# Layer 0 of a four-layer graph network: relation rows of three slots in four by one-hot matmuls, wider compares, one strided sum

## The chip, the cores and the metric

The kernel runs on one core of one Trainium2 chip, as one launch. The metric is the device time in microseconds. The engines and their names in the profile are TensorE (PE, its weight loads PEld), VectorE (DVE), ScalarE (ACT), GpSimd (POOL) and SyncE (SP). Each takes its own instructions in order; they meet at semaphores.

## What is computed

The reference is four graph layers in a row over 3125 nodes of 128 features and 100,000 edges sorted by target. After each of them the node features are added and normalized. The change is in layer 0, of which this is the core (`hP1` to `zWz` are small matrix products):

```python
z_edge = z[edge_type]                                  # 500 relations, 64 features
z_bar = segment_sum(z_edge, dst) / maximum(deg, 1)
pre_self = hP1 + hP2 + z_bar @ P3
pre_edge = hP1[dst] + hP2[src] + zP3[edge_type]
logits = leaky(pre) @ y_w                              # 8 heads, of edges and of nodes
alpha = softmax of the logits over all that arrive at one node
t_edge = hWh[src] + zWz[edge_type]
out = leaky(segment_sum(alpha * t, dst) + residual_weight * h)
```

So each edge needs a row that belongs to its source (`hP2`, `hWh`) and a row that belongs to its relation (`zP3`, `zWz`, and `z` itself for the mean). Layer 1 is a mean over neighbours, which the kernel computes with a matrix of edge counts; those counts are made inside layer 0's loop.

## The kernel before

**Tiles and slots.** The nodes are ordered by falling degree and cut into 25 tiles of 128, one node to a partition. Tile t has `CAP[t]` slots, 57 down to 21, 821 in all; a slot is one incoming edge of each of the 128 nodes. Slots are worked in chunks of up to W = 8, so a tile has some whole chunks and mostly a partial one, 114 in all.

**A chunk.** Both kinds of chunk first gather, by GpSimd, one row of 264 numbers per edge from `h_tab` into `hs` (L90, called at L824 and L841; one indirect DMA a slot; `hs` has 8 buffers). Then they differ:

- `gathered` (L819): GpSimd gathers a second row of 328 numbers per edge from `z_tab` into `zs` (two buffers). VectorE adds it to `hs` (L826), sums the relations' 64 features over the slots by halves (L814, L817) and adds the sum to `za` (L828). TensorE then builds the argument `pre` of the logits by matmuls with the identity (L799, L833).
- `multiplied` (L837): SyncE loads the relation numbers of 8 slots, repeated over the partitions, into `rb` (L843, two buffers). For each half of the chunk and each of the NK = 4 groups of 128 relations VectorE compares 512 columns with the group's relation numbers (L852), which makes a one-hot `oh`. TensorE multiplies it with `zq`, the relation table as a sum of three bf16 parts (L854, two matmuls for each one-hot, one PSUM buffer `zps`). ScalarE copies the result to `zT` (L856). TensorE adds it to `pre` (L858), adds `hs` (L860), and makes the value part `t_ps` three slots at a time (L866, one PSUM buffer); VectorE adds that to `hs` (L867). At the end VectorE sums `zT` over the 8 slots by halves (L870, L814, L817) and adds it to `zbT` (L874).

In both, `logits` copies `pre` with a ReLU (L806, ScalarE) and multiplies by `yw8` (L808).

**Which chunk is of which kind.** `by_matmul` (L68) takes n whole chunks of a tile, spread evenly, with n/full near 9/20 of all slots: 47 chunks, for instance the first and the third of four. 445 slots are gathered.

**End of a tile.** VectorE masks the logits (L881), takes the softmax, and `spread` (L885) weighs each chunk's `hs` and sums it; only then are the tile's `hs` buffers free. A chain of small steps closes the tile: the row x1 is scattered by GpSimd to `x1_tab` (L93) and `u` is written to `u_tab` (L1008).

**Counts.** `counts` (L563) is a generator whose steps are woven between the chunks: VectorE makes pairs of one-hots `c_ohs` and `c_ohd` (L559) for a piece of 512 columns, TensorE multiplies them block by block (L634) into `c_ps`, ScalarE copies it (L636). `NB[t]`, the blocks of ends per 128 columns, is 3 in the first 3 tiles, 2 in the next 21 and 1 in the last; a piece has 4 x NB blocks, at most SE = 12.

**Order.** The program's order within a queue is not quite that of the code: the framework lays the instructions out. In the trace the GpSimd queue holds the `hs` gathers of several chunks one after the other, then the load of x, the scatter of x1, and then the `zs` gathers.

Of the kernel before, what the change touches and what calls it, by code (L numbers as in the profile page):

```python
# [8 lines left out]
F32 = mybir.dt.float32  # L9
F16 = mybir.dt.float16  # L10
BF16 = mybir.dt.bfloat16
I32 = mybir.dt.int32
AF = mybir.ActivationFunctionType
OP = mybir.AluOpType
AX = mybir.AxisListType
# [3 lines left out]
P = 128  # L19
# [8 lines left out]
W = 8  # L28
# [6 lines left out]
R = 64  # L35
HC = 2 * D + H
NK = (PADREL + 1) // P
# [3 lines left out]
CAP = [57, 42, 40, 39, 38, 37, 36, 35, 35, 34, 33, 33, 32, 31, 31, 30, 30, 29, 28, 28, 27, 26, 25, 24, 21]  # L41
# [9 lines left out]
NB = [3] * 3 + [2] * (NT - 4) + [1]  # L51
CW = 512
# [15 lines left out]
def by_matmul(t):  # L68

    full = CAP[t] // W  # L70
    n = (9 * CAP[t] + 10 * W) // (20 * W)
    return {i * full // n * W for i in range(n)}


# [1 line left out]
def tile_gnn(ctx, tc, a, out):  # L76
    nc = tc.nc
    V, A, G, T = nc.vector, nc.scalar, nc.gpsimd, nc.tensor
# [10 lines left out]
    def gather(dst, table, idx, **kw):  # L89
        return G.indirect_dma_start(out=dst, out_offset=None, in_=table, in_offset=indirect(idx), **kw)  # L90
# [35 lines left out]
    relid = const.tile([P, NK], F32, name="relid")  # L126
# [223 lines left out]
    zq = slots.tile([P, NK, 4 * R], BF16, name="zq")  # L350
# [135 lines left out]
    with tc.tile_pool(name="srcp", bufs=1) as sp, tc.tile_pool(name="srcq", bufs=2, space=PSUM) as ps:  # L486
# [8 lines left out]
        for t in range(NT):  # L495
# [6 lines left out]
                                   op0=OP.add, op1=OP.mult)  # L502
            V.scalar_tensor_tensor(srcs[:, sl], pay_sb[:, sl, 0], float(-NP), live[:, :CAP[t]],
                                   op0=OP.add, op1=OP.mult)
# [10 lines left out]
        for o in range(0, NS, P):  # L515
            n = min(P, NS - o)
# [15 lines left out]
        blk0[nb] = late.tile([P, NT], F32, name=f"blk0_{nb}")  # L532
        G.iota(blk0[nb], pattern=[[nb * P, NT]], base=0, channel_multiplier=0, allow_small_or_imprecise_dtypes=True)
    SG = 8
    SE = max(NB) * CW // P
    each_j = slots.tile([P, NT, max(CAP)], BF16, name="each_j")
    V.tensor_copy(each_j, digits[:, :NT].unsqueeze(2).to_broadcast([P, NT, max(CAP)]))
    NAX = NT * max(NB)
# [1 line left out]
    def count_up(pool, ps):  # L540

        up = ps.tile([P, P, 2], BF16, name="c_up")
        of = up.rearrange("p d s -> p (d s)")
        ri = pool.tile([P, 1], I32, name="c_ri")
        V.tensor_copy(ri, rowid)
        V.tensor_scalar(ri, ri, 1, None, op0=OP.arith_shift_right)
        rf = pool.tile([P, 1], F32, name="c_rf")
        V.tensor_copy(rf, ri)
        for k in range(2):
            row = pool.tile([P, P], BF16, name="c_row", bufs=2)  # L550
            V.tensor_scalar(row, onesb, rf, float(k * P // 2), op0=OP.mult, op1=OP.add)
            T.transpose(of[:, k * P:(k + 1) * P], row, identb)
        return up

    def one_hots(to, nums, n, up):

        for i, k, w in ((0, n // 2, 2), (n - n % 2, n % 2, 1)):
            if k:
                V.tensor_tensor(to[:, i // 2:i // 2 + k, :, :w], nums[:, i:i + k * w]  # L559
                                .rearrange("p (b w) -> p b w", w=w).unsqueeze(2).to_broadcast([P, k, P, w]),  # L560
                                up[:, :, :w].unsqueeze(1).to_broadcast([P, k, P, w]), op=OP.is_equal)

    def counts(t, cp, ps, up):  # L563


        n, nb = CAP[t], NB[t]
        NA = NT * nb
        sl = slice(OFF[t], OFF[t + 1])
        oh = cp.tile([P, NT * max(CAP)], BF16, name="c_oh")[:, :NT * n]
# [7 lines left out]
        end = cp.tile([P, NT + 1], F32, name="c_end")  # L577
# [24 lines left out]
        for s0 in range(0, n, SG):  # L602
            k = min(SG, n - s0)
# [11 lines left out]
            for s in range(k):  # L615
                T.matmul(perm, ohb[:, s // 2, :, s % 2], oha[:, s].rearrange("p e a -> p (e a)"), start=(s0 + s == 0),
                         stop=(s0 + s == n - 1))
        ends = cp.tile([P, 2, NAX + NAX % 2], BF16, name="c_ends")
# [2 lines left out]
        cs = cp.tile([P, NP], BF16, name="c_sb")  # L621
        for c in range(NCW):
            w = min(CW, NP - c * CW)
            n2, e0 = nb * w // P, nb * CW // P * c
            yield
            ohs = cp.tile([P, SE // 2, P, 2], BF16, name="c_ohs", bufs=2)
            ohd = cp.tile([P, SE // 2, P, 2], BF16, name="c_ohd", bufs=2)
            for to, end in ((ohs, 0), (ohd, 1)):
                one_hots(to, ends[:, end, e0:e0 + n2], n2, up)
            cps = ps.tile([P, CW], F32, name="c_ps")  # L630
            for j in range(w // P):
                for i in range(nb):
                    b = nb * j + i
                    T.matmul(cps[:, j * P:(j + 1) * P], ohd[:, b // 2, :, b % 2], ohs[:, b // 2, :, b % 2],  # L634
                             start=(i == 0), stop=(i == nb - 1))
            A.activation(cs[:, c * CW:c * CW + w], cps[:, :w], AF.Copy)  # L636
        yield
        od_ps = ps.tile([P, NT], F32, name="c_od", tag="c_ps")
# [115 lines left out]
    with tc.tile_pool(name="l0", bufs=2) as wp, tc.tile_pool(name="l0s", bufs=1) as sp, \  # L754
# [40 lines left out]
        def argument(hq, k):  # L795

            pre = ps.tile([P, 4, P], F32, name="pre")
            for i in range(3):
                T.matmul(pre[:, :k], hq[:, i, :], identb.unsqueeze(1).to_broadcast([P, k, P]), start=(i == 0),  # L799
                         stop=False)  # L800
            return pre

        def logits(pre, k, lg_ps):

            low = wp.tile([P, 4, P], F32, name="low")
            A.activation(low[:, :k], pre[:, :k], AF.Relu)  # L806
            for s in range(k):
                T.matmul(lg_ps[:, s, :], low[:, s, :], yw8, start=True, stop=True)  # L808

        def halved(v, n, last=None):  # L810

            while n > 2:
                k = n // 2
                V.tensor_add(v[:, :k], v[:, :k], v[:, n - k:n])  # L814
                n -= k
            if n == 2:
                V.tensor_add(v[:, 0] if last is None else last, v[:, 0], v[:, 1])  # L817
# [19 lines left out]
        def multiplied(hq, o, n, zbT, first, lg_ps):  # L837

            hs = wp.tile([P, W, HC], F32, name="hs", bufs=8)
            for s in range(n):  # L840
                gather(hs[:, s, :], h_tab, srcx[:, o + s:o + s + 1])  # L841
            rb = wp.tile([P, W * P], F16, name="rb")
            nc.sync.dma_start(rb[:, :n * P], rel_tab[o:o + n].rearrange("(o s) p -> o (s p)", o=1)  # L843
                              .to_broadcast([P, n * P]))
            zT = wp.tile([P, W * P], F32, name="zT")
            for s0 in range(0, n, 4):
                k = min(4, n - s0)
                cols = slice(s0 * P, (s0 + k) * P)
                oh = wp.tile([P, NK, 4 * P], BF16, name="oh")[:, :, :k * P]
                zps = ps1.tile([P, 4 * P], F32, name="zps")[:, :k * P]  # L850
                for i in range(NK):
                    V.tensor_scalar(oh[:, i], rb[:, cols], relid[:, i:i + 1], None, op0=OP.is_equal)  # L852
                    for k2 in range(2):
                        T.matmul(zps, zq[:, i, 2 * R * k2:2 * R * (k2 + 1)], oh[:, i], start=(i + k2 == 0),  # L854
                                 stop=(i == NK - 1 and k2 == 1))
                A.activation(zT[:, cols], zps, AF.Copy)  # L856
                pre = argument(hq, k)
                T.matmul(pre[:, :k], zw[:, :D], zT[:, cols], start=False, stop=False)  # L858
                for s in range(k):
                    T.matmul(pre[:, s, :], hs[:, s0 + s, :D], ident, start=False, stop=(s == k - 1))  # L860
                logits(pre, k, lg_ps[:, s0:s0 + k])
            for s0 in range(0, n, 3):
                k = min(3, n - s0)
                t_ps = ps1.tile([P, 3, HC - D], F32, name="t_ps")
                for s in range(k):
                    T.matmul(t_ps[:, s, :], zT[:, (s0 + s) * P:(s0 + s + 1) * P], zw[:, D:], start=True, stop=True)  # L866
                V.tensor_add(hs[:, s0:s0 + k, D:], hs[:, s0:s0 + k, D:], t_ps[:, :k])  # L867
            assert n == W
            zh = wp.tile([P, W // 2, P], F32, name="zh")
            V.tensor_add(zh, zT.rearrange("z (s p) -> z s p", p=P)[:, :W // 2],  # L870
                         zT.rearrange("z (s p) -> z s p", p=P)[:, W // 2:])
            halved(zh, W // 2, zbT if first else None)
            if not first:
                V.tensor_add(zbT, zbT, zh[:, 0])  # L874
            return hs

        def masked(lg_ps, hss, n, mk):
# [28 lines left out]
        up = count_up(cp, ps1)  # L906

        def all_counts():
            for t in range(NT):
                yield from counts(t, cp, ps1, up)  # L910
# [6 lines left out]
        for t in range(NT):  # L917
            n = CAP[t]
# [5 lines left out]
            zbT = wp.tile([P, P], F32, name="zbT")  # L924
            hss = []
            mults = by_matmul(t)
            for s0, w in chunks(t):
                o = OFF[t] + s0
# [83 lines left out]
    with ExitStack() as ctx1, tc.tile_pool(name="l1", bufs=2) as wp, tc.tile_pool(name="l1s", bufs=1) as sp:  # L1012
# [14 lines left out]
        with tc.If(general > 0):  # L1027

            with tc.tile_pool(name="l1g", bufs=1) as gp, tc.tile_pool(name="l1gp", bufs=1, space=PSUM) as ps:
# [13 lines left out]
                for t in range(NT):  # L1043
# [27 lines left out]
                    for c in range(NCW):  # L1071
                        w = min(CW, NP - c * CW)
# [5 lines left out]
                for c in range(NCW):  # L1078
                    w = min(CW, NP - c * CW)
# [24 lines left out]
        for c in range(NCW):  # L1104
            w = min(CW, NP - c * CW)
# [11 lines left out]
            for i in range(w // P):  # L1117
                j = c * (CW // P) + i
# [26 lines left out]
    with tc.tile_pool(name="l2", bufs=2) as wp, tc.tile_pool(name="l2s", bufs=1) as sp, \  # L1145
# [100 lines left out]
        for t in range(NT):  # L1246
            qp = query(ps1, qb[:, t, :])
            for s0, s1, run in segments(t):
# [5 lines left out]
                n, o = s1 - s0, OFF[t] + s0  # L1254
# [46 lines left out]
    with tc.tile_pool(name="l3", bufs=2) as wp, tc.tile_pool(name="l3s", bufs=1) as sp, \  # L1301
# [28 lines left out]
        for t in range(NT):  # L1330
            n = CAP[t]
# [38 lines left out]
```

## Time and profile before

| what | value |
|---|---|
| median of 3 runs | 4815.34 us (4812.5 to 4819.78) |
| the profiled execution, its own time | 5636.56 us |
| its span, first to last instruction | 5634.8 us |
| mean granted TensorE clock in it | 0.619 |

The profiled execution is a run of its own and takes longer than the others. The span falls into five stages; the busy times are microseconds:

| from, to (us) | what | PE | DVE | ACT | POOL |
|---|---|---|---|---|---|
| 0, 330 | tables, order of the nodes, first gathers | 154 | 185 | 42 | 105 |
| 330, 2865 | layer 0, the loop over tiles | 1370 | 1337 | 647 | 1327 |
| 2865, 3080 | layer 1 | 146 | 54 | 26 | 30 |
| 3080, 4390 | layer 2 | 350 | 742 | 151 | 801 |
| 4390, 5635 | layer 3 | 6 | 642 | 62 | 806 |

How to read the profile: a group line has source line, engine, operation, output and inputs by the program's names with their shapes and a count; then busy microseconds and the mean nanoseconds of one; then the engine's idle time just before these instructions and what ended most of it. In the stage table each busy time is followed by the number of instructions, and the last columns are the granted TensorE clock, the DMA engines' busy share and GB/s. A wait line has the engine and what waited, what ended the wait, and then total microseconds, times, and the longest.

### The profile page before, as it was taken

What the parts mean: (1) busy time and instruction counts of PE and PEld (TensorE: products, weight loads), DVE (VectorE), ACT (ScalarE), POOL (GpSimd) and SP (SyncE); (2) the same over time, 40 slices, a digit from 0 to 9 for tenths busy, and PEclk for the clock granted to TensorE, in tenths of its full rate; (3) what the DMA queues carried; (4) which work ended last, traced back from release to release, by engine and by line L of the source; (5) the groups of instructions that cost most, each with busy time, mean ns of one, the idle gap of its engine ahead of it and who ended that gap; (6) DMA issues with size and microseconds to landing.
All of it is one profiled execution on the core that took longest, in us unless ns stands there. A gap on an engine that the chain in (4) does not pass through costs nothing. (4 is left out here: it accounts for less than half of the span.)

```text
span 5634.8 us, 37936 instructions
## 1 busy us (share of the span) xinstructions
PE 2025.8 (36%) x10974; PEld 1311.2 (23%) x11061; DVE 2959.0 (53%) x6784; ACT 927.9 (16%) x2462; POOL 3069.7 (54%) x3137
## 2 busy tenths in 40 slices
PE   7164554556544555555564022222233100000000
PEld 5143433334333444334432010111111000000000
DVE  8354664555544655555432455555566354555555
ACT  1032222222222322222111011111111000000000
POOL 0545566454554445444503756666564476666665
PEclk9576766666676777776677555555555555555555
DMA  2423333332233333323343333333332233333322
GB/s 82 124 73 91 93 93 96 86 90 75 77 91 84 83 86 88 89 82 84 101 170 119 105 96 105 104 103 114 98 109 84 81 100 91 89 89 95 94 85 68
DMA packets 220244, 530.70 MB, mean 94 GB/s; under 512 B 65689, under 2 KB 112460, under 8 KB 215385
## 3 DMA queue, kind: packets, MB, share of 16 engines
q0 software_dynamic: 147968, 437.97, 27.6%
q1 hardware_dynamic: 72024, 89.90, 4.9%
q8 instruction: 94, 1.54, 0.1%
q14 instruction: 158, 1.29, 0.1%
HBM read 457.09 MB, written 70.63 MB: 94 GB/s over the span
## 5 line engine op out<-in xcount | busy, mean ns | idle before, releaser
L90 POOL DMA_INDIRECT hs<-h_tab,srcx x821 | 880.3, 1072 | 666.2 <-issue 534.7
L90 POOL DMA_INDIRECT kv<-kv_tab,pay_sb x821 | 783.6, 954 | 423.9 <-issue 241.1
L90 POOL DMA_INDIRECT kv<-ktv_tab,pay_sb x821 | 780.2, 950 | 336.0 <-issue 256.1
L90 POOL DMA_INDIRECT zs<-z_tab,rel x445 | 458.0, 1029 | 451.6 <-DVE az L828 141.6
L706 DVE TENSOR_REDUCE u<-msg 128x128 f32<-128x1024 f32 (+4 forms) x228 | 384.3, 1686 | 114.5 <-remote 61.6
L808 PE MATMUL lg<-yw,low 128*128 128x8 f32 x1642 | 243.5, 274 | 126.2 <-ACT low L806 72.2
L634 PE MATMUL c_ps<-c_ohs,c_ohd 128*128 128x128 bf16 x1300 | 139.5, 264 | 406.3 <-issue 193.9
L808 PEld LDWEIGHTS lg<-yw,low 128*128 128x128 f32 x1642 | 235.5, 218 | 173.0 <-ACT low L806 107.1
L1315 DVE TENSOR_TENSOR qk<-kv,qp 128x1024 f32<-128x1024 f32 (+4 forms) x114 | 126.5, 1110 | 279.4 <-DMA kv<-ktv_tab,pay_sb 257.4
L559 DVE TENSOR_TENSOR c_ohs<-c_ends,c_up 128x1024 bf16<-128x1024 bf16 (+4 forms) x178 | 113.2, 637 | 296.1 <-remote 251.0
L612 ACT ACTIVATE c_oha<-c_oha,srclo 128x50 bf16<-128x50 bf16 (+2 forms) x821 | 201.4, 327 | 355.6 <-DVE c_oha L608 270.1
L854 PE MATMUL zps<-oh,zq 128*128 128x512 bf16 x677 | 237.7, 466 | 49.4 <-DVE oh L852 21.4
L702 DVE TENSOR_TENSOR msg<-kv,ex 128x1024 f32<-128x1024 f32 (+4 forms) x228 | 249.3, 1105 | 0.0
L866 PE MATMUL t_ps<-zw,zT 128*128 128x136 f32 x752 | 153.3, 340 | 212.9 <-DVE hs L867 128.2
L1163 DVE TENSOR_TENSOR qk<-kv,qp 128x1024 f32<-128x1024 f32 (+4 forms) x114 | 126.1, 1107 | 183.2 <-DMA kv<-kv_tab,pay_sb 175.6
L634 PEld LDWEIGHTS <-c_ohd 128*128 128x128 bf16 x1300 | 114.0, 118 | 431.8 <-issue 333.0
L799 PE MATMUL pre<-identb,hq 128*128 128x512 bf16 (+3 forms) x645 | 203.3, 414 | 5.0 <-issue 4.1
L636 ACT ACTIVATE c_sb<-c_ps 128x512 bf16<-128x512 f32 (+1 forms) x175 | 96.3, 550 | 653.8 <-remote 441.9
L717 PE MATMUL tp<-ident,xk 128*128 128x128 f32 x100 | 43.6, 436 | 432.7 <-DVE xk L1231 131.2
L806 ACT ACTIVATE low<-pre 128x512 f32<-128x512 f32 (+1 forms) x215 | 123.1, 574 | 406.3 <-remote 140.3
L826 DVE TENSOR_TENSOR hs<-hs,zs 128x2112 f32<-128x2112 f32 (+7 forms) x67 | 132.6, 1979 | 102.9 <-issue 43.8
L866 PEld LDWEIGHTS t_ps<-zw,zT 128*128 128x128 f32 x752 | 130.1, 234 | 239.2 <-DVE hs L867 137.5
(398 smaller groups left out, 5183.8 us busy)
## 6 DMA issues: line engine op xcount, KB each, us to landing
c_tab<-c_sb SPq DMA_DIRECT2D x25, 768.0 KB
cs<-c_tab SPq DMA_DIRECT2D x6, 3200.0 KB
hs<-h_tab,srcx POOLq DMA_INDIRECT x821
kv<-kv_tab,pay_sb POOLq DMA_INDIRECT x821
kv<-ktv_tab,pay_sb POOLq DMA_INDIRECT x821
rb<-rel_tab SPq DMA_DIRECT2D x47, 256.0 KB
zs<-z_tab,rel POOLq DMA_INDIRECT x445
h_tab<-h SPq DMA_DIRECT2D x25, 132.0 KB
```

The lines of the kernel that those rows point to most:

```text
L90: return G.indirect_dma_start(out=dst, out_offset=None, in_=table, in_offset=indirect(idx), **kw)
L612: A.activation(oha[:, s, 0, :], oha[:, s, 1, :], AF.Copy, scale=srclo[:, o:o + 1])
L634: T.matmul(cps[:, j * P:(j + 1) * P], ohd[:, b // 2, :, b % 2], ohs[:, b // 2, :, b % 2], start=(i == 0), stop=(i == nb - 1))
L702: V.tensor_tensor(msg[:, :n, :].rearrange("p s (h d) -> p s h d", h=heads), val.rearrange("p s (h d) -> p s h d", h=heads), ex.unsqueeze(3 ...
L706: V.tensor_reduce(u, msg[:, :n, :].rearrange("p s d -> p d s"), AX.X, OP.add)
L799: T.matmul(pre[:, :k], hq[:, i, :], identb.unsqueeze(1).to_broadcast([P, k, P]), start=(i == 0), stop=False)
L808: T.matmul(lg_ps[:, s, :], low[:, s, :], yw8, start=True, stop=True)
L826: V.tensor_add(hs[:, :n], hs[:, :n], zs[:, :n, :HC])
L854: T.matmul(zps, zq[:, i, 2 * R * k2:2 * R * (k2 + 1)], oh[:, i], start=(i + k2 == 0), stop=(i == NK - 1 and k2 == 1))
L866: T.matmul(t_ps[:, s, :], zT[:, (s0 + s) * P:(s0 + s + 1) * P], zw[:, D:], start=True, stop=True)
L1163: V.tensor_mul(qk[:, :n], kv[:, :n, :D], qp.unsqueeze(1).to_broadcast([P, n, D]))
L1315: V.tensor_mul(qk[:, :n], kv[:, :n, :D], qp.unsqueeze(1).to_broadcast([P, n, D]))
```

## The change

- `by_matmul` takes n/full near 3/4, and the chunks that it picks are then, for instance, the first three of four.
- In `multiplied` the compares are made ahead of both halves, over all 1024 columns of the chunk, one for each of the 4 groups. The one-hots lie in a ring of NK + 2 = 6 buffers of 1024 columns; before, it was 2 buffers of 4 x 512.
- The sum of `zT` over the 8 slots is one reduction that reads with a step of 512 bytes, in place of an addition of halves and two or three more. It writes `zbT` itself the first time in a tile.
- In `counts` the one-hots of a piece are made in steps of at most SG = 8 blocks instead of up to 12: with three blocks a piece takes two steps of 6 blocks, with two or one it still takes one. The tiles `c_ohs` and `c_ohd` shrink from 12 blocks to 8.

```diff
 def by_matmul(t):
     full = CAP[t] // W
-    n = (9 * CAP[t] + 10 * W) // (20 * W)
+    n = (3 * CAP[t] + 2 * W) // (4 * W)
     return {i * full // n * W for i in range(n)}
...
-    SE = max(NB) * CW // P
...
         for c in range(NCW):
             w = min(CW, NP - c * CW)
-            n2, e0 = nb * w // P, nb * CW // P * c
             yield
-            ohs = cp.tile([P, SE // 2, P, 2], BF16, name="c_ohs", bufs=2)
-            ohd = cp.tile([P, SE // 2, P, 2], BF16, name="c_ohd", bufs=2)
-            for to, end in ((ohs, 0), (ohd, 1)):
-                one_hots(to, ends[:, end, e0:e0 + n2], n2, up)
             cps = ps.tile([P, CW], F32, name="c_ps")
-            for j in range(w // P):
-                for i in range(nb):
-                    b = nb * j + i
-                    T.matmul(cps[:, j * P:(j + 1) * P], ohd[:, b // 2, :, b % 2], ohs[:, b // 2, :, b % 2],
-                             start=(i == 0), stop=(i == nb - 1))
+            for j0 in range(0, w // P, SG // nb):
+                tiles = range(j0, min(w // P, j0 + SG // nb))
+                e0, n2 = nb * (CW // P * c + j0), nb * len(tiles)
+                ohs = cp.tile([P, SG // 2, P, 2], BF16, name="c_ohs", bufs=2)
+                ohd = cp.tile([P, SG // 2, P, 2], BF16, name="c_ohd", bufs=2)
+                for to, end in ((ohs, 0), (ohd, 1)):
+                    one_hots(to, ends[:, end, e0:e0 + n2], n2, up)
+                for j in tiles:
+                    for i in range(nb):
+                        b = nb * (j - j0) + i
+                        T.matmul(cps[:, j * P:(j + 1) * P], ohd[:, b // 2, :, b % 2], ohs[:, b // 2, :, b % 2],
+                                 start=(i == 0), stop=(i == nb - 1))
...
+            ohs = []
+            for i in range(NK):
+                oh = wp.tile([P, W * P], BF16, name="oh", bufs=NK + 2)
+                V.tensor_scalar(oh[:, :n * P], rb[:, :n * P], relid[:, i:i + 1], None, op0=OP.is_equal)
+                ohs.append(oh)
             zT = wp.tile([P, W * P], F32, name="zT")
             for s0 in range(0, n, 4):
                 k = min(4, n - s0)
                 cols = slice(s0 * P, (s0 + k) * P)
-                oh = wp.tile([P, NK, 4 * P], BF16, name="oh")[:, :, :k * P]
                 zps = ps1.tile([P, 4 * P], F32, name="zps")[:, :k * P]
                 for i in range(NK):
-                    V.tensor_scalar(oh[:, i], rb[:, cols], relid[:, i:i + 1], None, op0=OP.is_equal)
                     for k2 in range(2):
-                        T.matmul(zps, zq[:, i, 2 * R * k2:2 * R * (k2 + 1)], oh[:, i], start=(i + k2 == 0),
+                        T.matmul(zps, zq[:, i, 2 * R * k2:2 * R * (k2 + 1)], ohs[i][:, cols], start=(i + k2 == 0),
                                  stop=(i == NK - 1 and k2 == 1))
...
             assert n == W
-            zh = wp.tile([P, W // 2, P], F32, name="zh")
-            V.tensor_add(zh, zT.rearrange("z (s p) -> z s p", p=P)[:, :W // 2],
-                         zT.rearrange("z (s p) -> z s p", p=P)[:, W // 2:])
-            halved(zh, W // 2, zbT if first else None)
+            zh = zbT if first else wp.tile([P, P], F32, name="zh")
+            V.tensor_reduce(zh, zT.rearrange("z (s p) -> z p s", p=P), AX.X, OP.add)
             if not first:
-                V.tensor_add(zbT, zbT, zh[:, 0])
+                V.tensor_add(zbT, zbT, zh)
             return hs
```

## The prediction

> **What bounds the kernel now.** I read the page's first part, then the stage table (busy time of each engine in stretches), then the groups by form, GpSimd's waits and the timeline of one cycle. The change touches only the loop over 25 tiles of layer 0. It runs from 330 to 2865 us of the span: the first row below is that loop, the others cut one cycle of it into four.
>
> ```profile
> core 0: us, PE busy (x) PEld busy (x) DVE busy (x) ACT busy (x) POOL busy (x), PEclk, DMA share, GB/s
> 330.00:2865.00 2535.00, 1369.54 (x8460) 982.00 (x8530) 1337.48 (x3630) 646.63 (x1734) 1326.73 (x1265) 0.69 0.32 87
> 1525.00:1585.00 60.00, 27.84 (x158) 19.64 (x158) 34.98 (x100) 15.68 (x48) 41.85 (x37) 0.69 0.32 85
> 1585.00:1604.00 19.00, 0.00 (x0) 0.00 (x0) 0.00 (x0) 0.00 (x0) 14.43 (x16) 0.50 0.48 127
> 1604.00:1638.00 34.00, 29.54 (x221) 22.55 (x222) 24.64 (x60) 12.13 (x28) 0.30 (x1) 0.87 0.14 40
> 1638.00:1700.00 62.00, 31.03 (x185) 23.03 (x187) 33.30 (x90) 17.73 (x50) 38.33 (x37) 0.70 0.31 85
> ```
>
> No engine is full over the loop: TensorE (PE) 54%, VectorE (DVE) 53%, GpSimd (POOL) 52%. They take turns. From 1585 to 1604 GpSimd alone works: its 16 instructions are gathers of `zs`, and everybody waits for them. From 1604 to 1638 it does nothing, and TensorE and VectorE work off what had piled up. Its waits say for what it stands still:
>
> ```profile
> POOL hs L90 <- issue: 519.8, 724, 38.4
> POOL zs L90 <- DVE az L828: 122.3, 13, 19.1
> POOL zs L90 <- issue: 117.3, 384, 0.6
> ...
> POOL zs L90 <- DVE oh L852: 58.2, 7, 21.5
> ```
>
> "issue" with a longest of 0.6 us is the ordinary gap of 0.30 us between two gathers. The waits before `zs` that a VectorE instruction ended (az, oh, and, below these, has 22.4, c_end 20.2, c_bs 17.6, zh 17.3, c_posi 16.9, zbT 15.7) make 291 us: `zs` has two buffers, and VectorE has not yet emptied one. The wait of up to 38.4 us before `hs` is for one of its eight buffers, which the end of a tile frees. So the loop is a ring: gathers, then a burst of compute, then buffers come free.
>
> **What the Trainium skill says.** "TensorE: Matmul & The Clock Gate", Part 1 (the HAM clock gate): the clock is halved by default and activity releases it. The trace agrees: granted 0.50 in the empty stretch, 0.87 in the dense one. So added matmuls cost less where they come dense. "SBUF — State Buffer", Specifications (TRN2): reads that cross to a new 16-byte line each time pay a penalty. The trace agrees: the sum over a 512-byte step takes 1870 ns (L706, below), the one along the row of as many elements 1212 ns (L1316). The same page, Who interferes with whom: VectorE's two-port modes, which `tensor_scalar` can enter, block GpSimd for the whole instruction. The trace leaves it open: gathers have a median of 949 ns and a mean of 1079 and 1034, so at most about 150 us of lengthening in the loop has any such cause.
>
> **The change part by part.** These groups of the kernel before give the durations (busy total and mean ns of one; instructions overlap a little, so means overstate):
>
> ```profile
> L854 PE MATMUL zps<-oh,zq 128*128 128x512 bf16 x677 | 237.7, 466 | 49.4 <-DVE oh L852 21.4 <-issue 7.6 <-DVE c_dig L598 6.2
> ...
> L866 PE MATMUL t_ps<-zw,zT 128*128 128x136 f32 x752 | 153.3, 340 | 212.9 <-DVE hs L867 128.2 <-issue 71.1 <-DVE zs L814 8.8
> ...
> L858 PE MATMUL pre<-zT,zw 128*128 128x512 f32 x188 | 130.0, 780 | 114.5 <-issue 67.2 <-ACT zT L856 44.2 <-ACT c_oha L612 2.9
> ...
> L852 DVE TENSOR_SCALAR oh<-rb,relid 128x512 bf16<-128x512 f16 x376 | 120.5, 359 | 45.8 <-remote 42.9 <-PE zps L854 2.3 <-issue 0.6
> ...
> L826 DVE TENSOR_TENSOR hs<-hs,zs 128x2112 f32<-128x2112 f32 x45 | 105.8, 2351 | 27.8 <-DMA zs<-z_tab,rel 13.3 <-DMA hs<-h_tab,srcx 7.2 <-issue 7.0
> ...
> L870 DVE TENSOR_TENSOR zh<-zT 128x512 f32<-128x512 f32 x47 | 32.2, 685 | 9.6 <-ACT zT L856 9.6
> ...
> L706 DVE TENSOR_REDUCE u<-msg 128x128 f32<-128x1024 f32 x184 | 344.2, 1870 | 102.5 <-remote 59.7 <-issue 27.9 <-DVE msg L702 7.7
> ```
>
> The new formula for the share, worked through the 25 capacities, gives 77 multiplied chunks in place of 47: 30 chunks, 240 slots, move. Relation gathers fall from 445 to 205.
>
> (1) **GpSimd, removed.** In the timeline the 16 gathers from 1584.55 to 1603.36 start 1.254 us apart. 240 x 1.254 = **-301 us**. GpSimd's queue holds nothing new; what stands behind the relation gathers (next tile's `hs`, the write of x1) moves up.
>
> (2) **GpSimd's waits for `zs`.** A tile now has mostly one whole and one partial gathered chunk, as many as `zs` has buffers, so the 291 us have little reason left. What is late next is the ring of eight `hs`. I take half as coming back there: **-145 us** (ends: 0 and -291).
>
> (3) **TensorE, added.** 677 of 752 records of L854 are there, so its true total is 237.7 x 752/677 = 264; with 130 and 153 that is 547 us for 47 chunks, 11.6 us each. 30 x 11.6 = +349 us. The work needs no relation gather, and the new chunk order (the first ones multiplied, the gathered one late) puts it ahead of the wait for `zs`. Laying the timeline's rows over each other, GpSimd is gathering during some 1620 us of the loop and TensorE is idle in 904 of these, 56%. I hide 56% there and put 44%, **+154 us**, on the path (ends: 0 and all 349).
>
> (4) **VectorE.** Compares: 376 x 0.359 = 135 become 308 of 1024 columns. No row shows that size; "VectorE: DVE Perf Modes", The perf-mode tier table, gives 693 ns for 2048 columns in the fourfold mode, which agrees with four columns a cycle, 0.26 ns a column: estimate 0.359 + 0.133 = 0.49 us, sum 152, +17 (at half that rate +59; at no added time -24). Sums over messages: 47 x (685+415+284 ns) + 22 x 284 = 71 us become 77 x 1.870 + 52 x 0.284 = 159, +88; I take L706's row because both read steps of 512 bytes (with 1212 ns, +37). Adding `t_ps` (574+574+431 ns): 30 x 1.58 = +47. Removed for 30 gathered chunks: the add of `zs` 2351, its tree 416+288+217 and the add to `az` 218: 30 x 3.49 = -105. Counts: only the 3 tiles with three blocks change, 36 compares of 1536 columns (945) become twice as many of 768 (550): +6. Together +53 us busy; VectorE is idle in 55% of the gathering time, so **+24 us** on the path, +53 uncovered.
>
> (5) **Others at nothing.** ScalarE gets 60 more copies of 594 ns, 36 us, hidden by its being busy 26% of the loop; +36 uncovered. SyncE issues 30 more loads of 256 KB (0.32 us each on its queue, in front of loads of `az` and writes of `c_tab`); they are prefetched by two buffers, +10 without that. DMA carries 40 MB less and 8 MB more, of 531. A compare can wait for the ring of six one-hots; behind it on VectorE stand the adds that free `zs` and the spreads that free `hs`. The old ring held one chunk, the new one a chunk and a half, so I count nothing (ends -10 and +20). If the longer compares block GpSimd, +18 at most (150 x 17/135).
>
> **Sum:** -301 - 145 + 154 + 24 = -268. The profiled execution took 5636.6 us (span 5634.8), so 5368.6 in its own terms. The median without profile is 4815.34, 0.8543 of that; no view tells which instructions profiling stretches, so I scale the whole: 4586 us. If none of the gain shrank, 4547; if it shrank to 0.7 of itself, 4628.
>
> **Rivals.** *More falls away*: all `zs` waits go, and matmuls hide entirely: -301 - 291 + 24 = -568, 5069, scaled 4330. For it: between the u_tab writes at 993.8, 1908.8 and 2636.4 lie two runs of 8 tiles with 16 multiplied chunks each, but 147 and 106 gathered slots, in 915 and 728 us; solved for the two kinds, 4.6 us a gathered slot and 1.9 a multiplied one, 240 x 2.7 = 640 saved. Against it: TensorE would be 1719 of some 1970 us busy. *Nothing moves*: about two thirds of all added work (302 of 349 + 53 + 36) lands in stretches where GpSimd waits for buffers, and all `zs` waits return before `hs`: 4815. *Slower*: TensorE takes the place of the gathers. All 349 and VectorE's 53 come onto the ring (each multiplied chunk needs its compares, copies and `t_ps` adds in alternation, one buffer of `zps` and one of `t_ps`, so it can't run dense), and the waits return: -301 + 402 = +101, 5738, scaled 4901. It decides from where over 75% of the 402 is uncovered. For it: in the burst from 1604 to 1638 TensorE is already 87% busy. *The change not doing what it says*: the single strided sum costs more than the tree (1870 against 1384); that is in step 4.
>
> **How the numbers follow.** Forecast 4586 with its own range 4480 to 4760: chance 0.50. More falls away (4300 to 4480): 0.24. Nothing moves: 0.07. Slower (to 4920): 0.19. Below 4390 and above 4840 I leave out one in ten each. A measurement of this kernel can tell about 0.2% from no change. Faster 0.77, within 0.2% 0.04, slower 0.19.
>
> **What would show it.** Step 1: 205 gathers of `zs`, loop shorter than 2535. Step 2: hardly any VectorE-ended waits before `zs`; if they reappear before `hs`, by how much. Step 3: TensorE busy near 1720 us in the loop, granted clock above 0.69; if it is over 80% busy and the loop no shorter, the slower rival holds. Step 4: compares near 490 ns, the sum near 1870 ns. I am wrong if the `hs` waits grow by more than 300 us.

## The result, and the profile after

The kernel after takes 4944.38 us (median of 4 runs, 4938.98 to 4947.81), the kernel before beside it 4817.56: ratio 1.0261, 95% interval 1.0244 to 1.0279. It is slower, where 4586 was forecast, and 4944 lies outside the range. In some batches every execution, the kernel before's too, took about 17% longer (before 5600 to 5675 us, elsewhere 4800 to 4835), and the profile that the prediction started from is such an execution; so a ratio below is always taken to the kernel before in the same batch.

Below is the stage table of after, with the columns as before. Its first row is the loop, which now runs from 300 to 2425 us of a span of 4942.9; the others are one cycle of its later half, cut where the work changes hands.

```profile
core 0: us, PE busy (x) PEld busy (x) DVE busy (x) ACT busy (x) POOL busy (x), PEclk, DMA share, GB/s
300.00:2425.00 2125.00, 1481.64 (x9536) 1043.65 (x9536) 1398.98 (x3502) 678.37 (x1787) 1082.93 (x1022) 0.79 0.32 87
2080.00:2103.00 23.00, 17.90 (x148) 13.04 (x147) 20.78 (x55) 7.17 (x15) 18.43 (x16) 0.91 0.36 103
2103.00:2119.00 16.00, 10.71 (x48) 6.91 (x46) 0.47 (x3) 2.56 (x5) 12.07 (x15) 0.81 0.49 140
2119.00:2151.00 32.00, 25.55 (x150) 18.37 (x151) 27.07 (x74) 14.05 (x43) 3.17 (x3) 0.79 0.17 43
```

A second profile of the kernel before, an execution of 4809 us, is what after has to be held against. There the loop ends at 2290:

```profile
300.00:2290.00 1990.00, 1292.66 (x8368) 946.84 (x8438) 1329.44 (x3612) 640.53 (x1718) 1390.95 (x1265) 0.74 0.40 109
```

So the loop grew by 135 us, although GpSimd is busy 308 us less in it. No engine is full: TensorE is busy 70% of after's loop, VectorE 66%, GpSimd 51%. In the cycle, VectorE does next to nothing from 2103 to 2119 (0.5 us) while GpSimd gathers, and GpSimd little from 2119 to 2151 (3.2 us) while VectorE works. GpSimd's waits in after's loop:

```profile
POOL hs L90 <- issue: 422.0, 680, 37.4
POOL hs L90 <- PE c_perm L615: 130.3, 6, 54.8
POOL hs L90 <- PE pre L864: 103.5, 11, 41.6
...
POOL zs L90 <- issue: 52.3, 172, 0.3
```

The waits before `zs` that VectorE ended make 30 us here. The prediction counted 291 in the execution that it read, but they are only 58 in the one of 4809 us. Those before `hs` are longer and end elsewhere. All idle time before `hs` is in the group lines, before first and after second:

```profile
L90 POOL DMA_INDIRECT hs<-h_tab,srcx x773 | 868.1, 1123 | 365.4 <-issue 311.9 <-PE pre L833 22.3 <-PE c_ps L634 9.9
```

```profile
L90 POOL DMA_INDIRECT hs<-h_tab,srcx x764 | 837.6, 1096 | 876.9 <-issue 422.0 <-PE c_perm L615 130.3 <-PE pre L864 103.5
L858 PE MATMUL zps<-oh,zq 128*128 128x512 bf16 x1176 | 346.9, 411 | 16.6 <-DVE oh L849 16.5
L870 PE MATMUL t_ps<-zw,zT 128*128 128x136 f32 x1184 | 232.5, 334 | 262.9 <-DVE hs L871 250.5 <-DVE mf L973 7.5 <-DVE bn_sd L729 4.0
L862 PE MATMUL pre<-zT,zw 128*128 128x512 f32 x296 | 187.7, 720 | 19.5 <-ACT zT L860 18.6
L849 DVE TENSOR_SCALAR oh<-rb,relid 128x1024 bf16<-128x1024 f16 x290 | 135.3, 489 | 21.6 <-PE zps L858 21.1 <-DMA rb<-rel_tab 0.2
L874 DVE TENSOR_REDUCE zh<-zT 128x128 f32<-128x1024 f32 x50 | 94.7, 1895 | 7.6 <-ACT zT L860 7.6
```

365 us of idle time before `hs` became 877: the time that the gathers no longer take is spent waiting for buffers. The durations came out as forecast (compare 489 ns, sum 1895), and no matmul of the relations waits long for anything but VectorE.

**Who holds the buffers.** VectorE's waits for gathers, before and then after:

```profile
DVE hs L826 <- DMA zs<-z_tab,rel: 289.4, 22, 35.4
DVE hs L826 <- DMA hs<-h_tab,srcx: 79.0, 5, 36.5
```

```profile
DVE zs L815 <- DMA zs<-z_tab,rel: 293.3, 18, 34.1
DVE hs L827 <- DMA hs<-h_tab,srcx: 174.1, 13, 27.5
```

The timeline of the cycle shows how such a wait turns into one of GpSimd. VectorE's rows, then GpSimd's (start, duration, instruction, and in brackets the idle time before it and what ended it):

```profile
2103.10 0.22 DVE L1008 CAST u<-rest 128x128 bf16<-128x128 f32 x1
2118.85 0.98 DVE L827 TENSOR_TENSOR hs<-hs,zs 128x792 f32<-128x792 f32 x1 [15.52 <-DMA hs<-h_tab,srcx]
2119.75 0.28 DVE L1009 TENSOR_TENSOR u<-rest,u 128x128 bf16<-128x128 f32 x1
...
2150.53 0.28 DVE L893 TENSOR_TENSOR az<-az,hs 128x128 f32<-128x128 f32 x1
```

```profile
2115.94 0.94 POOL L90 DMA_INDIRECT hs<-h_tab,srcx  x1 [0.30 <-issue]
...
2122.44 0.95 POOL L90 DMA_INDIRECT zs<-z_tab,rel  x1 [0.30 <-issue]
2151.56 4.10 POOL L90 DMA_INDIRECT hs<-h_tab,srcx  x1 [28.17 <-issue]
```

At 2103 VectorE comes to the add of a partial chunk of three slots (792 = 3 x 264), the last of the *next* tile, and stands 15.5 us until that tile's last gather, issued at 2115.94, has landed. Behind it in VectorE's queue lies the end of *this* tile: its first chunk is summed at 2150.53, which frees the first `hs` buffer, and at 2151.56 GpSimd goes on after 28 us of standing still. The two engines work in turn instead of side by side.

The buffer numbers in the compiled programs' queues say how often this is so. I counted the gathered chunks whose first use of `zs` on VectorE stands ahead of the first `spread` of the tile before: 12 in before, 31 in after. I call these early first uses. In 12 of after's 31 it is the add to `hs` itself that stands early (all ahead of the thirteenth or a later tile's end), by 34 to 67 instructions; in the others it is the tree over the relations' features. The framework lays them out so; the code has them in order.

### The profile page after: what moved, and what is told of

Same layout as the page of the kernel before. It is cut to its first block, busy times and chain, and to the rows that moved or that the text cites. A ratio compares the mean times of both kernels' runs of the same rounds, so it can differ in the third digit from the quotient of the medians.

```text
span 4942.9 us, 39811 instructions
## 1 busy us (share of the span) xinstructions
PE 2134.2 (43%) x12141; PEld 1373.4 (28%) x12141; DVE 2992.8 (61%) x6658; ACT 958.9 (19%) x2522; POOL 2830.0 (57%) x2897
## 5 line engine op out<-in xcount | busy, mean ns | idle before, releaser
L858 PE MATMUL zps<-oh,zq 128*128 128x512 bf16 x1232 | 363.0, 411 | 16.6 <-DVE oh L849 16.5
L870 PE MATMUL t_ps<-zw,zT 128*128 128x136 f32 x1232 | 241.3, 333 | 287.8 <-DVE hs L871 275.4
L870 PEld LDWEIGHTS t_ps<-zw,zT 128*128 128x128 f32 x1232 | 205.5, 228 | 327.1 <-DVE hs L871 274.6
L809 PE MATMUL lg<-yw,low 128*128 128x8 f32 x1642 | 226.7, 263 | 92.7 <-ACT low L807 91.5
L90 POOL DMA_INDIRECT zs<-z_tab,rel x205 | 205.6, 1003 | 88.7 <-issue 57.4
L864 PEld LDWEIGHTS pre<-ident,hs 128*128 128x128 f32 x1232 | 181.1, 212 | 81.5 <-issue 68.7
L827 DVE TENSOR_TENSOR hs<-hs,zs 128x2112 f32<-128x2112 f32 (+7 forms) x37 | 62.1, 1678 | 233.0 <-DMA hs<-h_tab,srcx 174.1
L862 PE MATMUL pre<-zT,zw 128*128 128x512 f32 x308 | 194.2, 716 | 19.6 <-ACT zT L860 18.6
L815 DVE TENSOR_TENSOR zs<-zs 128x128 f32<-128x128 f32 (+3 forms) x54 | 17.1, 320 | 293.5 <-DMA zs<-z_tab,rel 293.3
L864 PE MATMUL pre<-ident,hs 128*128 128x128 f32 x1232 | 187.2, 297 | 9.7 <-DMA hs<-h_tab,srcx 9.6
```

The source lines that it names most:

```text
L858: T.matmul(zps, zq[:, i, 2 * R * k2:2 * R * (k2 + 1)], ohs[i][:, cols], start=(i + k2 == 0), stop=(i == NK - 1 and k2 == 1))
```

## The experiments

**The parts one by one.** `before_again` is the kernel before, profiled once more (it gave the lines above).

> The kernel before, unchanged, for a second profile. The first one lasted 5636 us where its timed runs take 4817. If that execution was an odd one, this profile lasts about 4817 us and its layer 0 loop about 2000 us (4817 less the other stages as the changed kernel's profile has them: 300 + 215 + 1080 + 1223). If profiling as such stretches this kernel, it lasts about 5600 us again.

4809.02 us, span 4807.3, loop 1990: profiling as such does not stretch this kernel, and the first profile was of an odd execution.

`share_alone` changes only the formula in the kernel before; `after_old_share` goes back on it in the kernel after; `after_tree` has the tree again:

```diff
-    n = (9 * CAP[t] + 10 * W) // (20 * W)
+    n = (3 * CAP[t] + 2 * W) // (4 * W)
```
```diff
-    n = (3 * CAP[t] + 2 * W) // (4 * W)
+    n = (9 * CAP[t] + 10 * W) // (20 * W)
```
```diff
-            V.tensor_reduce(zh, zT.rearrange("z (s p) -> z p s", p=P), AX.X, OP.add)
+            V.tensor_add(zh, zT.rearrange("z (s p) -> z s p", p=P)[:, :W // 2],
+                         zT.rearrange("z (s p) -> z s p", p=P)[:, W // 2:])
+            halved(zh, W // 2, zbT if first else None)
...
-                V.tensor_add(zbT, zbT, zh)
+                V.tensor_add(zbT, zbT, zh[:, 0])
```

> The kernel before with the new share alone (77 multiplied chunks in place of 47; compares of 512 columns, sum by halves, counts as before). Theory ring (multiplied work lies on the ring of gathers, compute and release, and the gathers saved do not): slower, 1.01 to 1.04. Theory vector edits (the share gains, the strided sum loses more): faster, 0.96 to 0.99.

> The changed kernel with the old share (47 multiplied chunks), so wide compares, strided sum and count steps alone. Theory ring: within 1% of before (0.99 to 1.01), since these move VectorE by some 20 us of busy time. Theory vector edits: slower, 1.02 or more.

> The changed kernel with the sum over messages by halves again, as before. 77 sums at 1384 ns in place of about 1895. Theory ring: 39 us of VectorE busy time less, of which about half shows, 1.020 of before. Theory vector edits: most of the loss is gone, 1.00 or below.

| kernel | us | ratio to before | early first uses | VectorE's waits for gathers, us |
|---|---|---|---|---|
| before | 4813.86 | 1 | 12 | 377 |
| share_alone | 4837.53 | 1.0046 (1.0032 to 1.0061) | 27 | 408 |
| after_old_share | 4839.15 | 1.0050 (1.0037 to 1.0063) | 19 | 424 |
| after_tree | 4851.60 | 1.0073 (1.0052 to 1.0094) | 29 | 449 |
| after, in its own batch | 4944.38 | 1.0261 (1.0244 to 1.0279) | 31 | 497 |

The last column adds up VectorE's wait lines that end in a gather of `hs` or `zs`, in the profiled execution. `share_alone` and `after_tree` lie between the ranges of their two theories, so both theories missed; `after_old_share` came out as the ring theory had it. Each part alone costs some 25 us and together they cost 127, so the parts don't add up: something that isn't a sum of durations decides. And the new share by itself, with its 240 gathers fewer, does not pay.

**What the gathers are worth, and the sum's length.** `fewer_gathers` takes the relation gathers from the 30 chunks, and adds no other work; they add their own `hs` where they would add `zs`. `sum_contiguous` lets the one reduction read along the row.

```diff
-                gather(zs[:, s, :], z_tab, rl[:, s:s + 1])
-            V.tensor_add(hs[:, :n], hs[:, :n], zs[:, :n, :HC])
+                if not dry:
+                    gather(zs[:, s, :], z_tab, rl[:, s:s + 1])
+            zr = hs if dry else zs
+            V.tensor_add(hs[:, :n], hs[:, :n], zr[:, :n, :HC])
...
```
```diff
-            V.tensor_reduce(zh, zT.rearrange("z (s p) -> z p s", p=P), AX.X, OP.add)
+            V.tensor_reduce(zh, zT.rearrange("z (p s) -> z p s", p=P), AX.X, OP.add)
```

> The kernel before, in which the 30 chunks that the new share moves gather no relation rows: their 240 relation gathers are left out, and the chunk adds its own hs to itself where it would add zs, so VectorE does the same instructions (the numbers are then not the reference's). It measures what the removed gathers are worth by themselves. The prediction's steps 1 and 2: 240 gathers of 1.254 us are on the path, so at least 250 us less than before (below 4565). The theory that the loop's first half is limited by the ring of eight hs buffers and only its second half by GpSimd (97% of it taken by gathers and their gaps there, with VectorE and TensorE at 82%): 40 to 110 us less, nearly all of it after the tenth tile, and idle time before hs instead of the rest.

> The kernel after with the one reduction reading its 1024 numbers along the row in place of a step of 512 bytes (it then sums other numbers than it should); the order of the instructions is the same. If the sums stand on the path of the ring, 77 times (1895 - 1212 ns) = 53 us or a little less come off after's 4944, and the tree's gain of 92 us is mostly the price of the step. If VectorE's idle time hides them, as the prediction had it for most of step 4, under 20 us come off, and the tree's gain came from the order that the framework gave it.

`fewer_gathers`: 4437.98, ratio 0.9208 (0.9184 to 0.9231), 384 us less than the 4821.78 beside it. So the gathers are worth all that the prediction said, and the theory that GpSimd limits only the second half falls. (Its queue has 2 early first uses in place of before's 12, so a part of the 384 may be order.) `sum_contiguous`: 4937.74, ratio 1.0248 (1.0221 to 1.0274), 7 us from after, though each sum fell from 1895 to 1208 ns, 77 x 0.69 = 53 us in all, in the same order of instructions. The sums' length is not on the path in this order. The tree's 92 us then most likely came from the order it led to: its early uses are only two fewer, 29 against 31, but VectorE's waits for gathers are 48 us shorter. That is argued from the two profiles and not tested.

**The order, in steps.** `gated` keeps all of after's work but makes the add of `zs` also read a column of ones that the tile before writes from its weighed sum, so from the second tile on the add cannot stand ahead of that tile's end. `gathered_first` works the gathered chunks of a tile first.

```diff
-            V.tensor_add(hs[:, :n], hs[:, :n], zs[:, :n, :HC])
+            V.scalar_tensor_tensor(hs[:, :n], hs[:, :n], gate, zs[:, :n, :HC], op0=OP.mult, op1=OP.add)
...
                 spread(ac, hs, lg[:, s0:s0 + w], w)
+            gate = wp.tile([P, 1], F32, name="gate")
+            V.tensor_scalar(gate, ac[:, 0:1], 0.0, 1.0, op0=OP.mult, op1=OP.add)
```
```diff
-            for s0, w in chunks(t):
+            in_turn = sorted(chunks(t), key=lambda c: c[0] in mults)
+            for at, (s0, w) in enumerate(in_turn):
...
```

> The kernel after, in which the add of zs to hs in a gathered chunk also reads a column of ones that the tile before makes when its hs are weighed and summed, so that VectorE can't stand at the next tile's add before it has freed this tile's hs (one small instruction more a tile). Theory of the order: from the twelfth tile on the add of the next tile's last chunk lies some 60 instructions ahead of this tile's spread, VectorE waits there for the last gather, and GpSimd then waits for the spread; without that the second half returns to before's pace, 50 to 130 us under after's 4944. Theory that VectorE and TensorE just have more to do than the time that the gathers leave: no gain, within 15 us of 4944 or above.

> The kernel after with the gathered chunks of a tile worked ahead of the multiplied ones, so their gathers are the first of a tile's. Theory of the order: an add that stands early on VectorE then waits for the first gathers of the next tile and not for the last: 40 to 130 us under after's 4944. Theory that VectorE and TensorE have too much to do: within 15 us of 4944.

`gated`: 4808.44, 0.9971 (0.9964 to 0.9979); `gathered_first`: 4894.59, 1.0158 (1.0130 to 1.0186). The one gate takes 136 us off after, a little more than expected; the other chunk order 50, with 34 early uses left. What is left in `gated` is in its profile: VectorE still waits at the tree over the relations' features, which reads only `zs` and has no gate.

```profile
DVE zs L815 <- DMA zs<-z_tab,rel: 319.4, 20, 33.0
```

So in `gated_both` the tree's first add reads the column too, which is now made among the steps that close the tile (30 early first uses become 0). It ran three times. In the first two batches before took about 5650 us; in the third it took what the forecasts had assumed.

```diff
-            V.tensor_add(hs[:, :n], hs[:, :n], zs[:, :n, :HC])
-            halved(zs[:, :, HC:], n)
-            V.tensor_add(za, za, zs[:, 0, HC:])
+            plus(hs[:, :n], hs[:, :n], zs[:, :n, :HC], gate)
+            halved(zs[:, :, HC:], n, gate=gate)
+            plus(za, zs[:, 0, HC:], za, gate if n == 1 else None)
...
+            gate = has[:, 2:3]
+            V.tensor_scalar(gate, ac[:, 0:1], 0.0, 1.0, op0=OP.mult, op1=OP.add)
```

> The kernel after with the column of ones read by every first use of zs in a gathered chunk: the add to hs, and the first add of the tree over the relations' features, which in the run with one gate still stood ahead of the tile before's spread in 30 places and where VectorE waited 319 us for gathers of zs. If that order is what eats the gain of the removed gathers (384 us by the run without them), most of it comes back: 4450 to 4650. If TensorE and VectorE just have that much more to do, it stays within 30 us of the one gate's 4808.

> The kernel after with both gates once more, since the runs of its first batch, the kernel before's too, took some 830 us more than elsewhere and after itself was not among them. Beside a kernel before of 4815: if the order that the framework gave eats the gain of the removed gathers, 4450 to 4700; if TensorE and VectorE have that much more to do, within 30 us of the one gate's 4808.

> The kernel after with both gates. Where before takes 4815: theory of the order 4450 to 4700, theory of more to do within 30 us of the one gate's 4808. Where before takes 5650: again 1.1% faster than it, and by the theory of the order 60 us or more under after.

> The kernel after, unchanged, beside the gated one on the same chip. Where before takes 4815 it is 2.6% slower than before. Where before takes some 5650, as in the batches of the gated kernels and in the profile that the prediction started from: if the order costs the same there, after is 60 to 140 us above the gated one, so within 1.5% of before; if the long waits of that state cover it, within 20 us of the gated one and 1% faster than before.

Side by side, where before takes 4816.68: after 4941.64, 1.0260 (1.0243 to 1.0277); `gated_both` **4470.61**, 0.9282 (0.9267 to 0.9298). The same work in another order is 471 us shorter, and is the fastest kernel here that does all of the work. The stage row of its loop in this third run, VectorE's longest waits for gathers, and GpSimd's gathers of `hs`:

```profile
300.00:1957.00 1657.00, 1409.28 (x9536) 994.15 (x9536) 1404.82 (x3529) 675.14 (x1787) 1132.28 (x1022) 0.87 0.41 112
```

```profile
DVE hs L823 <- DMA hs<-h_tab,srcx: 24.4, 1, 24.4
DVE hs L825 <- DMA hs<-h_tab,srcx: 18.4, 2, 11.3
```

```profile
L90 POOL DMA_INDIRECT hs<-h_tab,srcx x764 | 844.1, 1105 | 405.4 <-issue 232.3 <-PE c_perm L615 56.7 <-PE c_ps L635 53.4
```

VectorE's instructions and busy time are after's (3529 and 1405 us against 3502 and 1399), its waits for gathers fell from 497 to 50 us, GpSimd's idle time before `hs` from 877 to 405. TensorE and VectorE are now busy 85% of the loop, and the granted clock is 0.87. The row of `fewer_gathers`, without the added work, is only 27 us shorter:

```profile
300.00:1930.00 1630.00, 1222.36 (x8381) 892.91 (x8449) 1327.53 (x3607) 641.08 (x1719) 1182.26 (x1026) 0.81 0.40 109
```

With a gate the framework lays out the other queues anew too, so GpSimd's order could be the cause in place of VectorE's. The traces settle most of this: the sequence of GpSimd's gathers of `hs` and `zs` is the same in `gated`, `gated_both` and `fewer_gathers`, so it has no part in the 338 us from `gated` (4808) to `gated_both`. From after to `gated` that sequence changes too, and how much of these 136 us is VectorE's order alone is open.

The number of early uses is not the price: `gathered_first` has 34 of them and after 31, and `gathered_first` is the faster. The waits fit better. From `gated` (359 us of VectorE's waits for gathers) over before (377) and the three kernels of the table to `gathered_first` (456) and after (497), the times rise in the same order as the waits, from 4808 to 4944.

**In the longer executions.** The other gated kernels met only these: `before_gated` (before with the gates), `tree_gated` (`gated_both` with the tree), `share_gated` (share_alone with the gates), the first two also as repeats, and `half_matmuls`:

```diff
-                    for k2 in range(2):
+                    for k2 in range(1):
...
```

> The kernel before with the same gates (12 places in which VectorE stands at the next tile's zs ahead of the spread). Theory of the order: the kernel before has it in fewer places and mostly in its first half, so it gains less than after does: 20 to 120 us under 4815, and the gated after is the faster of the two by 100 us or more. If the gates themselves help whatever the share, both gain the same.

> The kernel before with both gates. If the gates help whatever the share, it gains here as much as the gated after; if VectorE's early stand costs before little, as the theory of the order says, it stays within 40 us of 4815.

> The gated after with the tree over the messages in place of the strided reduction. If the tree's 92 us came from the order that it led to, nothing is left of them here: within 20 us of the run with both gates. If the sums' length is on the path, 40 us (77 times 0.5) or more under it.

> The gated after with the tree in place of the strided sum. In its first batch it was 0.4% faster than with the strided sum (5570 against 5594). If the sums' length is on the path once the order is mended, again 20 us or more less than the run with both gates; if the tree's gain was one of order, within 10 us.

> The kernel before with only the new share, and the gates: compares of 512 columns, tree, count one-hots of up to 12 blocks. It differs from the tree's gated run by the wider compares (77 times 4 times (2 x 359 - 489 ns) = 71 us less of VectorE's busy time there) and the counts. If VectorE is the limit once the order is mended, it is 40 to 70 us slower than the tree's gated run; if TensorE or the ring of hs is, within 20 us of it.

> The kernel after with both gates and only the first of the two matmuls for each one-hot: 616 of 128x512 left out (the relation rows then lack their lower part). TensorE loses 616 times 0.41 = 253 us of busy time, VectorE and ScalarE nothing. If TensorE is what eats the gain of the gathers, 100 us or more come off the run with both gates; if it is VectorE's or the ring's alternation, under 50.

| kernel | us | ratio to before | repeat |
|---|---|---|---|
| gated_both | 5594.33 | 0.9898 (0.9870 to 0.9927) | 0.9886 (0.9867 to 0.9904) |
| before_gated | 5657.19 | 1.0007 (0.9994 to 1.0021) | 1.0019 (0.9999 to 1.0038) |
| tree_gated | 5570.36 | 0.9854 (0.9821 to 0.9886) | 0.9829 (0.9811 to 0.9847) |
| share_gated | 5594.16 | 0.9895 (0.9868 to 0.9921) | |
| half_matmuls | 5546.63 | 0.9833 (0.9808 to 0.9858) | |

Here the gated after gains 1.1% on before, not 7%. After itself was not among these runs, so what the order costs it here is not known: the 471 us are shown only where before takes about 4815. `half_matmuls`, with 616 matmuls fewer, is 36 us under `gated_both` of its batch (5582.13), of 616 x 0.417 = 257 us of TensorE's time: TensorE's added work was mostly hidden there, under the 50 us forecast for the case that TensorE is not the limit. Gates don't help the kernel before in these executions; beside a before of 4815 it was not run, so what its own 12 early uses cost is open. The tree is 24 and 32 us faster than the strided sum under the gates; by the intervals only the second of these is clear. The first lies between the two forecasts made for it, and the second has the size that was forecast for sums whose length is on the path. So with the gates, and in these executions, the length seems to count. `share_gated` is 24 us slower than `tree_gated`, between its two forecasts (within 20, or 40 to 70), and decides nothing.

## Why the prediction was wrong, point by point

The main rival of the experiments, that VectorE and TensorE simply have more to do than the gathers leave time for, fails where before takes 4815: `gated_both` does that work within 33 us of `fewer_gathers` (4471 against 4438, two batches). The way from before to after can be laid over these kernels: -384 for the gathers, +33 for the work in their place, +471 for the order make +120, where +127 was measured. Such a chain of differences must close but for the drift between batches, so it is an account and no proof. The -384 is not the gathers alone either, as `fewer_gathers` has 2 early uses where before has 12.

- **Step 1** (-301) and **step 2** (-145), scaled, are -381, and `fewer_gathers` measured -384. That they agree is luck. Here are the gathers of `zs` of before (4809 us) and of `fewer_gathers`:

```profile
L90 POOL DMA_INDIRECT zs<-z_tab,rel x445 | 490.0, 1101 | 182.9 <-issue 122.6
L97 POOL DMA_INDIRECT zs<-z_tab,rel x205 | 251.6, 1227 | 66.5 <-issue 51.8
```

  The gathers and the gaps between them ("issue") fell by 309 us, which is step 1 as it stood, without the scaling; the other waits before `zs` fell by 46 (60 to 15), not by 145. Step 2 had read the waits of its own execution, and scaling made step 1 too small by 44.
- **Step 3** (+349 busy, 154 of it on the path) was too dear. Reckoned as there, its three groups grew by about 280; TensorE's busy time in all grew by 189, since other matmuls got shorter too (`c_ps` 258 to 238 ns), and in `gated_both` by 117. That dense work is clocked higher is what the Trainium skill says in "TensorE: Matmul & The Clock Gate", Part 1 (the HAM clock gate), and these rows agree: granted 0.74, 0.79 and 0.87 where TensorE is busy 65%, 70% and 85% of the loop. On the path, all added work of steps 3 and 4 costs 33 us in the gated order, not 178.
- **Step 4** (+53 busy, 24 on the path) was near: +70 busy, compares 489 ns for an estimate of 490, sums 1895 for 1870; nothing of the sums' length was on the path in after's order. The gathers did not get longer beside the longer compares: one of `hs` took 1123 ns before and 1096 after.
- **The step that failed** is the sentence in step 3 that the new chunk order, "the first ones multiplied, the gathered one late", puts added work "ahead of the wait for `zs`", together with step 5's count of nothing for what stands behind a waiting instruction on VectorE (it had only a compare in view). Both took the queue to follow the code. In the queue the late chunk's first use came ahead of the tile before's end, and its wait held up that tile's buffers. Taking this order away is worth 471 us, about twice the whole forecast gain of 229. With it gone the kernel takes 4471 us, just below the forecast's range.
- **The profile** hid it. In the 5636 us execution VectorE's 45 adds of full chunks (L826, shown in the prediction) waited 27.8 us; in the 4809 us one they waited 271.8:

```profile
L826 DVE TENSOR_TENSOR hs<-hs,zs 128x2112 f32<-128x2112 f32 x45 | 106.1, 2358 | 271.8 <-DMA zs<-z_tab,rel 226.0 <-DMA hs<-h_tab,srcx 34.8 <-issue 11.1
```

  All of VectorE's waits for gathers were 59 us in the first and 377 in the second, so the profile I reasoned from showed little of the wait that decides, and scaling a sum does not bring it back.
- The rival *slower* had the sign and about the size (4901), but not the cause: TensorE is busy 70% of after's loop, not over 80%. The mark "I am wrong if the `hs` waits grow by more than 300 us" looked at the right place: from the 4809 us execution they grew by 512. But from the execution that the prediction read, where they were 651, they grew by 226 only, so against its own profile the mark would have stayed silent. The mark of step 1, a loop shorter than 2535 us, was met by a slower kernel for the same reason.

## What to carry to other kernels

When a framework lays out the queues, a change of chunk order is a change of every engine's order: look in the queue, by buffer number, for an instruction of the next tile that waits for a transfer and has this tile's buffer release behind it. A dependency that costs next to nothing (a column of ones from the tile before; VectorE busy 1405 us against 1399) mends it. Weigh such places by the waits that they cause, not by their number. Hold a profile's span against the median before you reason from its waits; if it is 17% off, its waits are of another execution.

## What the runs showed that was not expected

The longer executions differ in waits more than in work: in the two profiles of before a matmul of `c_ps` takes 264 and 258 ns and a gather of `hs` 1072 and 1118, but TensorE's weight loads for `c_ps` had 431.8 us of idle time before them, most of it put down to nothing that the profile shows, in place of 110.9, longer execution first:

```profile
L634 PEld LDWEIGHTS <-c_ohd 128*128 128x128 bf16 x1300 | 114.0, 118 | 431.8 <-issue 333.0 <-DVE c_ohd L559 74.1 <-DVE az L992 6.7
```

```profile
L634 PEld LDWEIGHTS <-c_ohd 128*128 128x128 bf16 x1300 | 109.8, 116 | 110.9 <-DVE c_ohd L559 79.3 <-issue 22.3 <-DVE bn_sd L728 0.6
```

What holds TensorE there is open.
